# Transposing the gathered rows of routed expert tiles by DMA in two 16-bit planes, and the last 32 rows of an output projection as one stacked float32r product

## The chip, the cores and the metric

The kernel runs on one core of one Trainium2 chip. Its time is the device time of an execution in microseconds; lower is better. The engines are PE (TensorE), DVE (VectorE), ACT (ScalarE), POOL (GpSimd) and SP (SyncE, which here only issues transfers). L-numbers are lines of the kernel before.

## The reference, cut to what matters

There are N = 625 rows of D = 1024 float32 numbers and 20000 edges. A graph layer comes first, then an expert layer:

```python
# graph layer, on h = layernorm(x), n = t5_layer_norm(h)
out = n @ W_root + bias
for r in range(2):                        # mean of the messages of each relation
    sums = segment_sum((n[src] @ W_rel[r]) * (type == r)[:, None], dst)
    out += sums / maximum(count, 1)[:, None]
x = x + h + elu(out) @ wo                 # wo: 286 x 1024, the output projection

# expert layer, on h2 = layernorm(x)
shared = mean over 2 of  gelu(h2 @ sW1 + sb1) @ sW2 + sb2
moe    = sum over the top 2 of 8 experts of  w_e * (gelu(h2 @ W1[e] + b1[e]) @ W2[e] + b2[e])
x = x + h2 + shared + moe
```

The rows choose their experts by a gate computed at run time, so which rows meet which weights is known only then.

## The kernel before, in words

**Graph part.** Rows stand in NT = 5 tiles of TP = 125. PE counts the edges into a matrix (`cnt`), multiplies the normed rows by the three 286-column weights (`project`, L907), and aggregates by the counts (`aggregate`, L924, whose operands are float32r). `count_out` writes the counts with ACT copies. `elu(d)` makes a tile of activations of 286 columns, `elu_columns(d)` transposes it on PE into `eT`.

**Output projection.** `output_proj(d)` (L962) multiplies `eT` by `wo`. The first 256 rows of `wo` go as two float32 products per 512-column half (L967). The remaining 30 rows go as a pair of 30-row products, one for each half (L971), at two different row offsets of the array. DVE then adds the result to `xh` (L974), takes its statistics, and scales it (`layernorm`, L729; its square root is on ACT, L721) into `h2`. POOL issues the DMAs that store `h2` to the DRAM tensor `h2d` and `xh` to `x1d` (L980, L981). `to_columns(d)` transposes `h2` on PE (L808) and ACT copies the transposes to `h2T` (L816). The loop of L1070 emits `output_proj(s)` and then `to_columns(s - 2)`.

**Routing.** While PE multiplies the shared experts' first weights (`shared_in`, L1163), DVE finds for each row its two experts and the slot it takes. The result `tok` (L1282) lists, for each of NJ = 11 tiles of 128 slots, which row sits in each slot. `bias_parts` uses a buffer of the pool `io`, called `b2x`.

**Routed experts, first product.** The loop of L1409 runs over the 11 tiles. `fetch(j)` has POOL gather the 128 rows of a tile from `h2d` into `xs` (pool `io`, 3 buffers), PE transposes the eight 128x128 blocks into PSUM (`p_x`, L1366), and ACT and DVE copy four blocks each to `xsT` (L1372, L1370; pool `xt`, 2 buffers). `expert_in(j)` multiplies (`p_h`, L1385); DVE copies the result to `hj`. `expert_mid(j)` transposes that on PE (`p_hT`, L1397) and ACT applies gelu into `hjT` (L1400). PE's order is: transposes of tile n+1, product of tile n, transposes of `hj` of tile n-1. ACT also makes copies of weights, `w1m` (L1379), for tiles that hold more than one expert.

**The rest.** The second product of the routed experts (`p_yj`, L1443), a scatter of its rows to DRAM, the shared experts' second product (`p_o`, L1498), the sum and the stores. Pools are given back and reused as the stages end: the pool `xt` lies where the shared experts' inputs were.

Of the kernel before, what the change touches and what calls it, by code (L numbers as in the profile page):

```python
# [18 lines left out]
N = 625  # L19
D = 1024  # L20
# [433 lines left out]
def sparse_kernel(  # L454
# [32 lines left out]
    banks_of = ExitStack()  # L487
    psum, nacc = [banks_of.enter_context(tc.tile_pool(name="psum", bufs=1, space=bass.MemoryType.PSUM))], [3]
    dram = ctx.enter_context(tc.tile_pool(name="dram", bufs=1, space=bass.MemoryType.DRAM))
    h2d = dram.tile([N, D], F32, name="h2d")  # L490
    x1d = dram.tile([N, D], F32, name="x1d")

    yt = dram.tile([2 * YB, D], F32, name="yt")
# [17 lines left out]
    crow = pool(cnts, "crow", 2)  # L511
    front = ExitStack()
    fbig = pool(front, "fbig", side="right")
    oneh = pool(front, "oneh", 6, side="right")


    PARTS = (slice(0, 112), slice(112, TP))
# [303 lines left out]


    CT = cbig.tile([TP, NT, R * N], F32R, name="CT")
    def count_out(d, n, acc):
        xi = crow.tile([TP, R * WD], I32, tag="xi", name=f"xi_{d}")[:, : R * n]
        nc.scalar.activation(xi, acc[:, : R * n], AF.Copy, scale=256.0)
        five = [TP, NT, R * n]
        ct = crow.tile([TP, NT, R * WD], I32, tag="ct", name=f"ct_{d}")[:, :, : R * n]
        nc.vector.tensor_tensor(ct, xi[:, None, :].to_broadcast(five),
                                mask[:, :, None].to_broadcast(five), op=ALU.bitwise_and)  # L830
        for r in range(R):
            nc.scalar.copy(CT[:, :, r * N + d : r * N + d + n], ct.rearrange("p t (d r) -> p t d r", r=R)[:, :, :, r])

# [66 lines left out]
    agg = gbig.tile([TP, NT, F], F32, name="agg")  # L900


    def project(i):
        r, m = divmod(i, NT)
        p = ps_acc(f"p_pr_{m}_{r}")
        for k in range(KD):
            nc.tensor.matmul(p[:TP, :F], nT[:, k, m * TP : (m + 1) * TP], wg[:, k, r, :],  # L907
                             start=(k == 0), stop=(k == KD - 1))
        if r < R:
            rest = crow.tile([TP, F], F32, tag="rest", name=f"rest_{m}_{r}")  # L910
            nc.scalar.activation(rest, p[:TP, :F], AF.Copy, scale=sc2[:, 1, m : m + 1])
            nc.scalar.copy(P[:, m, r, 0, :F], rest)
            nc.vector.tensor_sub(P[:, m, r, 1, :F], rest, P[:, m, r, 0, :F])
        else:
            nc.vector.scalar_tensor_tensor(agg[:, m, :], p[:TP, :F], sc2[:, 0, m : m + 1], cb,
                                           op0=ALU.mult, op1=ALU.add)

    def aggregate(d, r):

        p = (ps_acc if r and d in (1, 3, 4) else ps_mm)(f"p_agg_{d}_{r}")  # L920
        at = r * N + d * TP
        for m in range(NT):
            for i in range(2):
                nc.tensor.matmul(p[:TP, : F + 2], CT[:, m, at : at + TP], P[:, m, r, i],  # L924
                                 start=(m == 0 and i == 0), stop=(m == NT - 1 and i == 1))
        nc.scalar.copy(deg[:, R * d + r : R * d + r + 1], p[:TP, F : F + 1])
        inv = small.tile([TP, 2], F32, tag="inv", name=f"inv_{d}_{r}")
        nc.vector.tensor_scalar(inv[:, 0:1], p[:TP, F : F + 1], 1.0, None, op0=ALU.max)
        nc.vector.reciprocal(inv[:, 1:2], inv[:, 0:1])
        nc.vector.scalar_tensor_tensor(agg[:, d, :], p[:TP, :F], inv[:, 1:2], agg[:, d, :],  # L930
                                       op0=ALU.mult, op1=ALU.add)

    els = {}

    def elu(d):
        z = agg[:, d, :]
# [12 lines left out]
    def elu_columns(d):  # L949
        p = ps_mm(f"p_elT_{d}")  # L950
        pv = p[:, : 3 * TP].rearrange("p (k n) -> p k n", k=3)
        eT = grow.tile([128, 3, TP], F32, tag="eT", name=f"eT_{d}", bufs=NT - 1)
# [5 lines left out]
        eTs[d] = eT  # L958

    h2s = {}  # L960

    def output_proj(d):  # L962
        eT = eTs[d]
        ps = [ps_acc(f"p_y_{d}_{s}") for s in range(2)]
        for s in range(2):
            for k in range(2):
                nc.tensor.matmul(ps[s][:TP, :], eT[:, k, :], wo_t[:, k, s * 512 : (s + 1) * 512],  # L967
                                 start=(k == 0), stop=False)
        for s in range(2):
            r = slice(s * QC, s * QC + FL)  # L970
            nc.tensor.matmul(ps[s][:TP, :], eT[r, 2, :], wo_r[r], start=False, stop=True)  # L971
        for s in range(2):
            at = slice(s * 512, (s + 1) * 512)
            nc.vector.tensor_add(xh[:TP, d, at], xh[:TP, d, at], ps[s][:TP, :])  # L974
# [25 lines left out]
    def at(c, f, *args):  # L1000
        after[c].append((f, args))
# [3 lines left out]
            at(c0, stats, t + 1)  # L1005
        at(c1, to_columns, t + 1, None, nT, True)

    zero = fbig.tile([128, D // 2], F32, name="zero")

    def clear():  # L1010
        nc.gpsimd.memset(zero, 0.0)
        for a in range(2):
# [341 lines left out]
    xsT, p_hs, w1m = {}, {}, {}  # L1354

    def fetch(j):
        xs = io.tile([128, D], F32, tag="io", name=f"xs_{j}")
        nc.gpsimd.indirect_dma_start(  # L1358
            out=xs, out_offset=None, in_=h2d,
            in_offset=bass.IndirectOffsetOnAxis(ap=tok[:, j : j + 1], axis=0))  # L1360
        t_ = xt.tile([128, KD, 128], F32, tag="xsT", name=f"xsT_{j}")
        for g in range(2):
            p = ps_acc(f"p_x{g}_{j}")
            for k in range(4):
                at = (4 * g + k) * 128
                nc.tensor.transpose(p[:, k * 128 : (k + 1) * 128], xs[:, at : at + 128], ident)  # L1366
# [182 lines left out]
```

## Time and profile before

| | |
|---|---|
| median of 3 runs | 298.02 us (296.13 to 298.16) |
| the profiled execution's own time | 298.92 us |
| its span, first to last instruction | 297.2 us |
| mean granted TensorE clock | 0.994 |
| PE busy, of the span | 286.6 us, 96% |
| DVE, ACT, POOL busy | 166.1, 102.0, 43.9 us |
| output projection and its transposes | 97.3 to 131.2 us of the span |
| shared experts' first product | to 165.0 us |
| routed experts' first product | 165.0 to 216.0 us |
| bytes moved by DMA in that last stage | 84 GB/s on the mean |

The profile is of one execution. Its page gives busy times, a picture of the span in 40 slices, the chain of work that ended last, and groups of equal instructions. The chain can also be read piece by piece, with the start, the length and the line of each piece. A group's row gives the line, the engine, what is written from what, the count, the busy time with the mean of one, and the idle time of the engine before them with what ended it. In the chain a float32 matmul counts as two PE instructions.

### The profile page before, as it was taken

What the parts mean: (1) busy time and instruction counts of PE and PEld (TensorE: products, weight loads), DVE (VectorE), ACT (ScalarE), POOL (GpSimd) and SP (SyncE); (2) the same over time, 40 slices, a digit from 0 to 9 for tenths busy, and PEclk for the clock granted to TensorE, in tenths of its full rate; (3) what the DMA queues carried; (4) which work ended last, traced back from release to release, by engine and by line L of the source; (5) the groups of instructions that cost most, each with busy time, mean ns of one, the idle gap of its engine ahead of it and who ended that gap; (6) DMA issues with size and microseconds to landing.
All of it is one profiled execution on the core that took longest, in us unless ns stands there. A gap on an engine that the chain in (4) does not pass through costs nothing.

```text
span 297.2 us, 4546 instructions
## 1 busy us (share of the span) xinstructions
PE 286.6 (96%) x1583; PEld 190.7 (64%) x1583; DVE 166.1 (56%) x458; ACT 102.0 (34%) x236; POOL 43.9 (15%) x97
## 2 busy tenths in 40 slices
PE   7988999999999999999999999999999999999991
PEld 5866777788888434567777887788743334444451
DVE  6779999997664588838980222132133211157920
ACT  2338424413542322335132543646289111000000
POOL 9500000000000034322021221110012222200000
PEclk9999999999999999999999999999999999999997
DMA  6999920000000999999999433420086545399351
GB/s 218 333 311 391 408 87 1 3 0 2 0 0 23 342 366 394 392 390 375 356 409 409 163 112 125 131 82 2 2 306 247 210 192 225 138 354 370 136 156 45
DMA packets 28658, 61.01 MB, mean 205 GB/s; under 512 B 2177, under 2 KB 16008, under 8 KB 28625
## 3 DMA queue, kind: packets, MB, share of 16 engines
q1 hardware_dynamic: 23102, 43.77, 41.4%
q0 software_dynamic: 5232, 16.55, 15.1%
q10 hardware_dynamic: 296, 0.35, 0.5%
q8 instruction: 15, 0.25, 0.4%
q14 instruction: 13, 0.10, 0.1%
HBM read 42.62 MB, written 18.81 MB: 207 GB/s over the span
## 4 chain that ended last, share of the span: by engine, by line
PE 87%; DMA 4%; DVE 4%; ACT 2%; SPq 1%; issue 0%; ACTq 0%
PE p_pr L907 17%; PE p_h L1385 13%; PE p_yj L1443 13%; PE p_o L1498 12%; PE p_sh L1163 11%; PE p_y L967 6%; PE p_agg L924 5%; DMA xh<-in_x_dram 4%; PE p_x L1366 3%; PE p_y L971 2%; PE cnt L885 1%; PE p_t L808 1%; PE p_hT L1397 1%; DVE st L765 1%; PE p_gate L1111 1%; PE p_o L1500 1%
## 5 line engine op out<-in xcount | busy, mean ns | idle before, releaser
L907 PE MATMUL p_pr<-wg,nT 128*125 128x286 f32 x240 | 61.8, 409 | 1.4 <-ACT nT L814 0.9
L907 PEld LDWEIGHTS p_pr<-wg,nT 128*125 128x125 f32 x240 | 43.6, 187 | 14.1 <-ACT nT L814 2.2
L1385 PE MATMUL p_h<-w1a,xsT 128*128 (+2 forms) x176 | 40.0, 380 | 0.0
L1443 PE MATMUL p_yj<-w2a,hjT 128*128 (+2 forms) x88 | 38.6, 594 | 0.0
L1498 PE MATMUL p_o<-sw,shT 128*125 128x512 f32 (+1 forms) x88 | 36.1, 553 | 0.0
L1163 PE MATMUL p_sh<-h2T,sw 128*128 128x313 f32 (+1 forms) x128 | 35.2, 429 | 0.0
L1385 PEld LDWEIGHTS p_h<-w1a,xsT 128*128 128x128 f32 (+2 forms) x176 | 28.8, 168 | 7.4 <-issue 0.5
L1163 PEld LDWEIGHTS p_sh<-h2T,sw 128*128 128x128 f32 x128 | 23.7, 190 | 8.6 <-issue 0.2
L1443 PEld LDWEIGHTS p_yj<-w2a,hjT 128*128 128x128 f32 (+2 forms) x88 | 14.4, 168 | 22.4 <-issue 22.4
L1498 PEld LDWEIGHTS p_o<-sw,shT 128*125 128x125 f32 x88 | 16.4, 188 | 16.9 <-issue 16.2
L1447 DVE COPY ys<-p_yj 128x512 f32<-128x512 f32 x15 | 10.4, 692 | 28.7 <-PE p_yj L1443 27.1
L1389 DVE COPY hj<-p_h 128x256 f32<-128x256 f32 x11 | 4.7, 425 | 30.8 <-PE p_h L1385 30.8
L981 POOL DMA_DIRECT2D x1d<-xh x10 | 5.4, 539 | 94.4 <-DVE flagf L710 91.3
L1451 POOL DMA_INDIRECT yt<-ys,row x11 | 10.8, 981 | 50.5 <-DVE ys L1447 50.5
L967 PE MATMUL p_y<-wo_t,eT 128*125 128x512 f32 x40 | 18.0, 593 | 0.0
L1358 POOL DMA_INDIRECT xs<-h2d,tok x11 | 10.6, 962 | 45.6 <-PE p_x L1366 30.9
L1370 DVE COPY xsT<-p_x 128x512 f32<-128x512 f32 x11 | 7.6, 692 | 17.4 <-PE p_x L1366 14.7
L1400 ACT ACTIVATE hjT<-p_hT,vT 128x128 f32<-128x128 f32 (+2 forms) x34 | 8.7, 332 | 24.5 <-PE p_hT L1397 24.5
L1474 DVE SCALAR_TENSOR_TENSOR x<-p_o,x 125x512 f32<-125x512 f32 (+1 forms) x11 | 6.9, 641 | 16.3 <-PE p_o L1500 16.3
L924 PE MATMUL p_agg<-P,CT 125*125 125x288 f32 x100 | 15.5, 305 | 0.0
L1385 PE MATMUL p_h<-w1m,xsT 128*64 128x256 f32 (+1 forms) x96 | 14.7, 382 | 0.0
L1443 PE MATMUL p_yj<-w2m,hjT 128*64 128x512 f32 (+1 forms) x48 | 14.1, 595 | 0.0
(306 smaller groups left out, 413.9 us busy)
## 6 DMA issues: line engine op xcount, KB each, us to landing
w1a<-in_L_ffn_W_dram SPq DMA_DIRECT2D x8, 1024.0 KB
w2a<-in_L_ffn_W_dram SPq DMA_DIRECT2D x8, 1024.0 KB, 7.0
yt<-zero SPq DMA_DIRECT2D x2, 2560.0 KB
g<-yt SPq DMA_DIRECT2D x10, 512.0 KB, 7.5
sw<-in_L_ffn_sW_dram SPq DMA_DIRECT2D x4, 1024.0 KB, 6.8
x<-x1d SPq DMA_DIRECT2D x5, 500.0 KB
x1d<-xh POOLq DMA_DIRECT2D x5, 448.0 KB, 6.6
h2d<-h POOLq DMA_DIRECT2D x5, 448.0 KB, 6.2
```

The source lines that it names most:

```text
L907: nc.tensor.matmul(p[:TP, :F], nT[:, k, m * TP : (m + 1) * TP], wg[:, k, r, :], start=(k == 0), stop=(k == KD - 1))
L924: nc.tensor.matmul(p[:TP, : F + 2], CT[:, m, at : at + TP], P[:, m, r, i], start=(m == 0 and i == 0), stop=(m == NT - 1 and i == 1))
L967: nc.tensor.matmul(ps[s][:TP, :], eT[:, k, :], wo_t[:, k, s * 512 : (s + 1) * 512], start=(k == 0), stop=False)
L1163: nc.tensor.matmul(p[:, : z - a], sw1[:, i, k, t * 128 : (t + 1) * 128], h2T[:, k, a:z], start=(k == 0), stop=(k == KD - 1))
L1358: nc.gpsimd.indirect_dma_start(out=xs, out_offset=None, in_=h2d, in_offset=bass.IndirectOffsetOnAxis(ap=tok[:, j : j + 1], axis=0))
L1366: nc.tensor.transpose(p[:, k * 128 : (k + 1) * 128], xs[:, at : at + 128], ident)
L1385: nc.tensor.matmul(p[a:b, :H], xsT[j][:, k, a:b], w1m[j, a][:, 0, k, :] if a else w1a[:, bass.ds(e, 1), k, :], start=(k == 0), stop=(k == ...
L1400: nc.scalar.activation(hjT[:, j, t, a:b], p[:, t * 128 + a : t * 128 + b], AF.Gelu, bias=bT[:, bass.ds(e, 1), t])
L1443: made = nc.tensor.matmul(p[a:b], hjT[:, j, k, a:b], w2m[j, a, k][:, at] if a else w2a[:, bass.ds(e, 1), k, at], start=(k == 0), stop=(k = ...
L1447: nc.vector.tensor_copy(y[:, at], p)
L1451: sent.append(nc.gpsimd.indirect_dma_start(out=yt, out_offset=bass.IndirectOffsetOnAxis(ap=row[:, j : j + 1], axis=0), in_=y, in_offset=No ...
L1498: nc.tensor.matmul(p[:TP, :n], shT[:, i, k, own], sw2[:, i, k, at], start=(i == 0 and k == 0), stop=False)
```

## The change

Three things are done together.

1. `h2d` holds each row as two 16-bit planes: ACT splits `h2` into low and high halves of its numbers (a new tile `hp`, two ACT copies per tile of 125 rows), and POOL stores `hp`. A gathered tile `xs` is then 128 rows of 2048 16-bit numbers. The SP queue transposes it with two DMA transposes per tile, of 1024 columns each, into `xq` (2 buffers). DVE copies the low plane of each half and ACT the high plane, interleaved, to `xsT`. PE's eight transposes per tile and their PSUM buffers go.
2. The last 32 rows of `wo` (254 to 285) are loaded four times below each other into a tile of 128 rows and split into float32r parts, once (`last_rows`, one ACT copy and one DVE instruction). `elu` repeats the last 32 columns, `elu_columns` makes a float32r tile `eR` of them, with a DVE subtraction for the lower 64 rows, and `output_proj` adds one float32r product of 128 rows per half in place of the 30-row product.
3. Buffers are given up for it: `io` has 2 instead of 3, `oneh` 5 instead of 6, `agg` is used for the four copies of the rows of `wo` before it holds sums, and `zero` is declared earlier.

```diff
-    h2d = dram.tile([N, D], F32, name="h2d")
+    h2d = dram.tile([N, 2 * D], I16, name="h2d")
-    oneh = pool(front, "oneh", 6, side="right")
+    oneh = pool(front, "oneh", 5, side="right")
...
-    FL = F - 256
+    FL = F - QC
     nc.sync.dma_start(wo_t, wo[:256].rearrange("(t p) m -> p t m", p=128))
-    wo_r = gbig.tile([2 * QC, 512], F32, name="wo_r")
-    for s in range(2):
-        nc.sync.dma_start(wo_r[s * QC : s * QC + FL], wo[256:, s * 512 : (s + 1) * 512])
+    agg = gbig.tile([128, NT, F], F32, name="agg")
+    wo_4 = agg.rearrange("p t f -> p (t f)")[:, :D]
+    nc.sync.dma_start(wo_4, bass.AP(tensor=wo.tensor, offset=wo.offset + FL * D,
+                                    ap=[[0, 4], [D, QC], [1, D]]))
+    wo_r = gbig.tile([128, D], F32R, name="wo_r")
+    less = fbig.tile([128, 1], F32, name="less")
+    for g in range(4):
+        nc.gpsimd.memset(less[g * QC : (g + 1) * QC], -float(g % 2))
+
+    def last_rows():
+        with tc.issue_after(outs[-1].ins):
+            nc.scalar.copy(wo_r, wo_4)
+        nc.vector.scalar_tensor_tensor(wo_r, wo_r.bitcast(F32), less, wo_4, op0=ALU.mult, op1=ALU.add)
...
     def elu(d):
...
-        el = grow.tile([TP, 256 + 2 * QC], F32, tag="el", name=f"el_{d}", bufs=3)
-        nc.vector.memset(el[:, 256:], 0.0)
+        el = grow.tile([TP, FL + 128], F32, tag="el", name=f"el_{d}", bufs=3)
...
-        nc.scalar.copy(el[:, 256 + QC : F + QC], el[:, 256:F])
+        nc.scalar.copy(el[:, F:].rearrange("p (g f) -> p g f", g=3),
+                       el[:, FL:F][:, None, :].to_broadcast([TP, 3, QC]))
...
     def elu_columns(d):
...
-        for k in range(3):
-            n = min(128, 256 + 2 * QC - k * 128)
-            nc.tensor.transpose(pv[:n, k, :], els[d][:, k * 128 : k * 128 + n], ident[:TP, :TP])
-        nc.scalar.copy(eT[:, :2], pv[:, :2])
-        nc.scalar.copy(eT[: 2 * QC, 2], pv[: 2 * QC, 2])
+        eR = grow.tile([128, TP], F32R, tag="eR", name=f"eR_{d}", bufs=NT - 1)
+        for k, a in enumerate((0, 128, FL)):
+            nc.tensor.transpose(pv[:, k, :], els[d][:, a : a + 128], ident[:TP, :TP])
+        nc.scalar.copy(eT, pv[:, :2])
+        nc.scalar.copy(eR, pv[:, 2])
+        nc.vector.tensor_sub(eR[64:], pv[64:, 2], eR[64:])
...
     def output_proj(d):
...
         for s in range(2):
+            at = slice(s * 512, (s + 1) * 512)
             for k in range(2):
-                nc.tensor.matmul(ps[s][:TP, :], eT[:, k, :], wo_t[:, k, s * 512 : (s + 1) * 512],
-                                 start=(k == 0), stop=False)
-        for s in range(2):
-            r = slice(s * QC, s * QC + FL)
-            nc.tensor.matmul(ps[s][:TP, :], eT[r, 2, :], wo_r[r], start=False, stop=True)
+                n = min(128, FL - k * 128)
+                nc.tensor.matmul(ps[s][:TP, :], eT[:n, k, :], wo_t[:n, k, at], start=(k == 0), stop=False)
+            nc.tensor.matmul(ps[s][:TP, :], eR, wo_r[:, at], start=False, stop=True)
...
         h2s[d] = h2
+        hp = planes.tile([TP, 2, 2, D // 2], I16, tag="hp", name=f"hp_{d}")
+        for g in range(2):
+            nc.scalar.copy(hp[:, g], h2[:, g * 512 : (g + 1) * 512].bitcast(I16).rearrange("p (d b) -> p b d", b=2))
         for g in PARTS:
             at = slice(d * TP + g.start, d * TP + g.stop)
-            nc.gpsimd.dma_start(h2d[at, :], h2[g, :])
+            nc.gpsimd.dma_start(h2d[at, :], hp[g].rearrange("p g b d -> p (g b d)"))
...
+    at(100, last_rows)
...
+            planes = pool(gnn, "planes", 2)
...
-    io = pool(ctx, "io", 3)
+    io = pool(ctx, "io", 2)
...
     def fetch(j):
-        xs = io.tile([128, D], F32, tag="io", name=f"xs_{j}")
+        xs = io.tile([128, 2 * D], I16, tag="io", name=f"xs_{j}")
         nc.gpsimd.indirect_dma_start(
             out=xs, out_offset=None, in_=h2d,
             in_offset=bass.IndirectOffsetOnAxis(ap=tok[:, j : j + 1], axis=0))
         t_ = xt.tile([128, KD, 128], F32, tag="xsT", name=f"xsT_{j}")
+        o = t_.bitcast(I16).rearrange("p k (n b) -> p b k n", b=2)
         for g in range(2):
-            p = ps_acc(f"p_x{g}_{j}")
-            for k in range(4):
-                at = (4 * g + k) * 128
-                nc.tensor.transpose(p[:, k * 128 : (k + 1) * 128], xs[:, at : at + 128], ident)
-            o = t_[:, 4 * g : 4 * g + 4, :]
-            pv = p.rearrange("p (k n) -> p k n", k=4)
-            if g:
-                nc.vector.tensor_copy(o, pv)
-            else:
-                copied = nc.scalar.copy(o, pv)
+            xq = xt.tile([128, 2, KD // 2, 128], I16, tag="xq", name=f"xq_{j}_{g}")
+            nc.sync.dma_start_transpose(xq.rearrange("p b k n -> p (b k) n"), xs[:, g * D : (g + 1) * D])
+            k = slice(4 * g, 4 * g + 4)
+            nc.vector.tensor_copy(o[:, 0, k], xq[:, 0])
+            copied = nc.scalar.copy(o[:, 1, k], xq[:, 1])
         xsT[j] = t_
```

More of the change, by code (lines that the diff above doesn't have):

```diff
@@ L655, in sparse_kernel @@
     wo_t = gbig.tile([128, 2, D], F32, name="wo_t")
-    FL = F - 256
+    FL = F - QC
     nc.sync.dma_start(wo_t, wo[:256].rearrange("(t p) m -> p t m", p=128))
-    wo_r = gbig.tile([2 * QC, 512], F32, name="wo_r")
-    for s in range(2):
-        nc.sync.dma_start(wo_r[s * QC : s * QC + FL], wo[256:, s * 512 : (s + 1) * 512])
+    agg = gbig.tile([128, NT, F], F32, name="agg")
[10 more added lines that the diff above has]
+        nc.vector.scalar_tensor_tensor(wo_r, wo_r.bitcast(F32), less, wo_4, op0=ALU.mult, op1=ALU.add)
+    zero = fbig.tile([128, 512], F32, name="zero")
     nc.vector.tensor_scalar(low[:, 1], low[:, 0], 1.0 / DEG, 0.5 / DEG - 0.5, op0=ALU.mult, op1=ALU.add)
@@ L823, in sparse_kernel @@
     CT = cbig.tile([TP, NT, R * N], F32R, name="CT")
+    outs = []
     def count_out(d, n, acc):
@@ L831, in count_out @@
         for r in range(R):
-            nc.scalar.copy(CT[:, :, r * N + d : r * N + d + n], ct.rearrange("p t (d r) -> p t d r", r=R)[:, :, :, r])
+            outs.append(nc.scalar.copy(CT[:, :, r * N + d : r * N + d + n],
+                                       ct.rearrange("p t (d r) -> p t d r", r=R)[:, :, :, r]))
     nil = fbig.tile([1, 512], BF16, name="nil")
@@ L899, in sparse_kernel @@
         nc.gpsimd.memset(P[:, m, :, 0, F:].bitcast(F32), 16.0 ** -m)
-    agg = gbig.tile([TP, NT, F], F32, name="agg")
     def project(i):
@@ L914, in project @@
         else:
-            nc.vector.scalar_tensor_tensor(agg[:, m, :], p[:TP, :F], sc2[:, 0, m : m + 1], cb,
+            nc.vector.scalar_tensor_tensor(agg[:TP, m, :], p[:TP, :F], sc2[:, 0, m : m + 1], cb,
                                            op0=ALU.mult, op1=ALU.add)
@@ L929, in aggregate @@
         nc.vector.reciprocal(inv[:, 1:2], inv[:, 0:1])
-        nc.vector.scalar_tensor_tensor(agg[:, d, :], p[:TP, :F], inv[:, 1:2], agg[:, d, :],
+        nc.vector.scalar_tensor_tensor(agg[:TP, d, :], p[:TP, :F], inv[:, 1:2], agg[:TP, d, :],
                                        op0=ALU.mult, op1=ALU.add)
@@ L935, in elu @@
     def elu(d):
-        z = agg[:, d, :]
+        z = agg[:TP, d, :]
         lo = grow.tile([TP, F], F32, tag="lo", name=f"lo_{d}")
@@ L951, in elu_columns @@
         pv = p[:, : 3 * TP].rearrange("p (k n) -> p k n", k=3)
-        eT = grow.tile([128, 3, TP], F32, tag="eT", name=f"eT_{d}", bufs=NT - 1)
-        for k in range(3):
-            n = min(128, 256 + 2 * QC - k * 128)
-            nc.tensor.transpose(pv[:n, k, :], els[d][:, k * 128 : k * 128 + n], ident[:TP, :TP])
-        nc.scalar.copy(eT[:, :2], pv[:, :2])
-        nc.scalar.copy(eT[: 2 * QC, 2], pv[: 2 * QC, 2])
-        eTs[d] = eT
+        eT = grow.tile([128, 2, TP], F32, tag="eT", name=f"eT_{d}", bufs=NT - 1)
+        eR = grow.tile([128, TP], F32R, tag="eR", name=f"eR_{d}", bufs=NT - 1)
[4 more added lines that the diff above has]
+        nc.vector.tensor_sub(eR[64:], pv[64:, 2], eR[64:])
+        eTs[d] = eT, eR
     h2s = {}
     def output_proj(d):
-        eT = eTs[d]
+        eT, eR = eTs[d]
         ps = [ps_acc(f"p_y_{d}_{s}") for s in range(2)]
         for s in range(2):
+            at = slice(s * 512, (s + 1) * 512)
             for k in range(2):
-                nc.tensor.matmul(ps[s][:TP, :], eT[:, k, :], wo_t[:, k, s * 512 : (s + 1) * 512],
-                                 start=(k == 0), stop=False)
-        for s in range(2):
-            r = slice(s * QC, s * QC + FL)
-            nc.tensor.matmul(ps[s][:TP, :], eT[r, 2, :], wo_r[r], start=False, stop=True)
+                n = min(128, FL - k * 128)
+                nc.tensor.matmul(ps[s][:TP, :], eT[:n, k, :], wo_t[:n, k, at], start=(k == 0), stop=False)
+            nc.tensor.matmul(ps[s][:TP, :], eR, wo_r[:, at], start=False, stop=True)
         for s in range(2):
@@ L1006, in sparse_kernel @@
         at(c1, to_columns, t + 1, None, nT, True)
-    zero = fbig.tile([128, D // 2], F32, name="zero")
     def clear():
```

## The prediction

> **What bounds the kernel now.** I read the page's busy times first, then its chain of work by engine.
>
> ```profile
> span 297.2 us, 4546 instructions
> PE 286.6 (96%) x1583; PEld 190.7 (64%) x1583; DVE 166.1 (56%) x458; ACT 102.0 (34%) x236; POOL 43.9 (15%) x97
> ...
> PE 87%; DMA 4%; DVE 4%; ACT 2%; SPq 1%; issue 0%; ACTq 0%
> ```
>
> PE is busy 96% of the span and is 87% of the chain: PE work taken out shortens the kernel only while nothing else falls in behind it. Next, the same chain piece by piece (start, length, piece) over the stage with the removed transposes:
>
> ```profile
> 159.77 5.26 PE p_sh L1163 x20
> 165.03 1.75 PE p_x L1366 x16
> 166.77 3.46 PE p_h L1385 x16
> 170.23 0.87 PE p_x L1366 x8
> 171.10 3.46 PE p_h L1385 x16
> 174.56 0.22 PE p_hT L1397 x2
> 174.78 0.87 PE p_x L1366 x8
> ...
> 212.05 3.59 PE p_h L1385 x64
> 215.64 0.37 PE p_hT L1397 x2
> 216.01 0.86 PE p_yj L1443 x2
> ```
>
> PE runs without a gap from 165.03 to 216.01. A tile costs 3.46 to 3.60 (`p_h`) + 0.87 (`p_x`) + 0.22 to 0.37 (`p_hT`), some 4.6 us.
>
> The third view is the chain over the output projection, and the fourth the timeline of DVE there:
>
> ```profile
> 117.63 1.00 PE p_t L808 x8
> 118.63 3.44 PE p_y L967 x8
> 122.07 1.10 PE p_y L971 x4
> ```
>
> ```profile
> 117.66 0.69 DVE L974 TENSOR_TENSOR xh<-xh,p_y 125x512 f32<-125x512 f32 x1 [0.56 <-PE p_y L971]
> ...
> 123.15 0.69 DVE L974 TENSOR_TENSOR xh<-xh,p_y 125x512 f32<-125x512 f32 x1 [0.50 <-PE p_y L971]
> ```
>
> PE needs 3.44 + 1.05 + 1.00 = 5.49 us per tile. DVE works on each tile for all but 0.16 to 0.56 us of that, so it stands close behind.
>
> **Output projection: cheaper on PE, then bound by DVE.** The 30-row pair costs 1.05 per tile. A float32r matmul of 288 columns takes 1.40/10 = 0.14 us in the chain (`p_agg`, L924), so one of 512 columns 0.14 x 512/288 = 0.25, and two 0.50. PE saves 0.55 x 5 = 2.8 us. The first tile gives its 0.55 in full; after that DVE's idle times before L974 are all that can be recovered: 0.16 + 0.28 + 0.56 + 0.50 = 1.5. That is 2.05. Against it stand ten new ACT copies `hp`, 2 per tile, of 1024 elements per partition; the nearest row, the bfloat16 copy of L646, takes 1.04. In the built program they stand on ACT ahead of the next tile's square root, for which DVE waits: `hp` of tile d starts once tile d-1 is copied to `h2T`, and 2.1 us later comes the square root. I lay this out tile by tile and find it 0.1 to 0.3 late on two tiles. I take 1.8 gained; bounds 0.5 (the copies late each time) and 2.8. The shared product then ends at 165.03 - 1.8 = 163.2 instead of 165.03. `h2d` is written 2 us later than `h2` was, at some 137, and is needed by the first gather at 149.2: covered by 10 us of `p_sh`.
>
> **One-time work: nothing.** `last_rows` (1.04 on ACT, 1.28 on DVE, by L1434 and L796), three memset-like edits, the wider copy in `elu`, the DVE subtraction on 64 rows in `elu_columns`, one `oneh` buffer less: all lie near 57 to 97 us, where PE's row stands at nine tenths or more and DVE's at four to nine. Without that cover it would be 2 us; I count 0, and -0.5 to +1 for the range.
>
> **Routed stage: what goes.** PE loses 11 x 0.87 = 9.6 us. With PE alone as bound the stage would end at 163.2 + (216.0 - 165.0 - 9.6) = 204.6.
>
> **What comes.** A tile now goes gather, two DMA transposes, copies, product. Three waits of the built program matter.
> (a) `xq` lies where the shared experts' inputs were: the first transpose waits for the last `p_sh` matmul, at 163.2. PE, which used to start `p_x` right there, waits for a whole transpose and a copy.
> (b) `xq` has two buffers, one tile's worth: a transpose of tile n+1 waits for the DVE and ACT copies of the same half of tile n.
> (c) `io` has two buffers: the gather of tile n+2 waits until both transposes of tile n are done. Queued behind it on POOL are only later gathers; behind a waiting transpose on SP only later transposes.
>
> The gather's own time is shown, from its issue:
>
> ```profile
> DMA to landing us min/median/max: 4.1/4.7/8.9
> ```
>
> With the semaphores around it I take 4.9. It was hidden by a third buffer: POOL's timeline has them issued 8 to 13 us ahead of their PE transposes.
>
> **Price of a transpose.** No row shows one. Call L the time from issue to landing of one half (128 x 1024 numbers of two bytes, 256 KB) and D the time by which the second half lands later. Low end for D: the bytes at the trace's best slice, 409 GB/s, 0.64 us. High end: the Trainium skill, VectorE: DVE Perf Modes, section "The three transpose paths", gives 1.309 us for one 128x128 block by DMA against 0.39 on TensorE, and its rules send 128x128 transposes to TensorE where PSUM will do. Eight such blocks in a row are 10.5 us. The row and that rule differ much: here a PE transpose of a float32 block costs 0.87/8 = 0.11 us. By the rule read serially the stage would take 11 x 21 us and the kernel near 480; by plain copy speed it would win. The nearest row is SP's own cost of issuing a transfer:
>
> ```profile
> 215.70 0.89 SPq L1422 DMA_DIRECT2D sw<-in_L_ffn_sW_dram  x2
> ```
>
> That is 0.445 each. A transpose here is 64 blocks of 16 rows by 128 columns. The skill (DMA: Bandwidth & Descriptors, in the table on descriptor generation, column for earlier generations) has 512 cycles for a plain transfer and 262,144 for 8,192 transposed blocks, 32 per block. By the trace's 0.445 us a cycle is 0.87 ns, so 64 blocks take 64 x 32 x 0.87 = 1.8 us. This is an estimate; no run shows it yet. I take **D = 1.8**. For L add the fixed part: a 448 KB store lands 3.3 us after issue, 1.1 of it bytes, so 2.1 with the issue. **L = 3.9, L + D = 5.7.**
>
> **The sum.** Wait (c) makes a ring over two tiles: 4.9 + 5.7 = 10.6, or 5.3 us per tile. Wait (b) alone gives L + 0.8 (copy and semaphore) = 4.7; PE alone 3.8. So (c) decides. Tile 0 is transposed at 163.2 + 5.7 = 168.9. Tiles 2, 4, 6, 8, 10 follow at 10.6 each: 221.9. The last tile's first half is there D earlier, 220.1; then copy 0.7, `p_h` 3.6, `p_hT` 0.4: 224.8. Before it was 216.0. The stage ends **8.8 us later**. In general the end is 163.2 + 29.2 + 6(L + D) - D; one us of L is worth six.
>
> DVE and ACT do one more copy of each half: 11 x (2 x 0.69) - 7.6 = +7.6 on DVE (12.1 busy of 51 before) and +6.5 on ACT (25.1 of 51), by L1370 and L1372. Both have room, and the copy's latency of 0.7 is in the sum. If a mode for 2-byte data makes it 0.35, ring (b) gains and (c) does not. PE will stand still for 4.7 us at 163; should its clock drop, `p_h` of tile 0 is longer by at most its own 3.5, and the second tile is not there before 173: covered.
>
> **After it.** The loads of `sw2` and `x1` start as the stage ends and are needed by `p_o` 38 us later, as before. The shift passes to the end whole: 298.92 + 8.8 = 307.7 for an execution like the profiled one, which lies 0.9 above the median of the runs; so **307 us**.
>
> **The rivals.**
> *Quick transposes (faster).* The pages also say (Advanced Engine Details and Errata, "X-Bar Transpose") that such DMAs run like plain ones. With D = 0.6 and L = 2.5 the end is 163.2 + 29.2 + 18.6 - 0.6 = 210.4, a gain of 5.6: **292.5**. It decides from L + D below 3.55, where the gain passes 3 us. For it speaks that the stage moves only 84 GB/s; against it, that L cannot be much under the 2.1 of fixed cost, and that each element lands in two bytes. Floor: PE alone, -11.4, 286.6. Chance 0.25.
> *Break-even.* L + D of 3.55 to 4.6 (D near 1): the freed PE time turns into waiting, 298 within 3 us. Chance 0.10; within 1% is what a measurement of this kernel can about tell from no change.
> *Slow transposes.* D = 3.5, L = 6 (75 GB/s): ring (c) gives 7.2 per tile, the two halves in line 7.0; end 163.2 + 29.2 + 57 - 3.5 = 245.9, kernel **328**. For it speaks the page's 1.309 us per block, against it that 64 blocks can be spread over 16 DMA engines. Chance 0.20.
> *The forecast's case*, L + D of 4.6 to 7.5, 301 to 318: 0.45.
> A rival of another kind, that PE's freed 0.87 is not on the path, is excluded by the gapless chain.
>
> **Range.** 291 to 335: below lie 1 in 20 cases (nearly perfect overlap), above 1 in 10 (L + D over 10.5). Slower by over 1%: 0.45 + 0.20 = 0.65; within 1%: 0.10; faster: 0.25.
>
> **What would show it.** After the last `p_sh` PE idles 4 to 5 us, waiting for a copy of `xsT`; then 1 to 2 us before each `p_h`. Gathers wait for DMA transposes, not for DVE or ACT, and come in step with them, 5.3 us apart. The transposes' landing time is L. `p_y` with the stacked product takes 3.9 per tile, and the last `p_sh` ends 1 to 2.5 us earlier. If PE has no gaps between tiles, the forecast is wrong by its price L + D; if the idle time before `p_h` ends on ACT or DVE copies that waited for buffers, the ring was misread.

## The result, and the profile after

| | before | after |
|---|---|---|
| median of 4 runs each, on one chip | 298.09 us (296.13 to 298.25) | 320.25 us (317.42 to 324.36) |
| ratio, 95% interval | | 1.073 (1.068 to 1.079) |
| profiled execution: own time, span | 298.92, 297.2 us | 320.70, 318.7 us |
| mean granted TensorE clock | 0.994 | 0.975 |
| first product of the routed experts | 165.03 to 216.01 | 158.69 to 237.04 |

The changed kernel is 7.3% slower. The ratio leaves out the changed kernel's slow run of 324.36 us. The forecast was 307 us, 3.0% slower: the direction holds, the size is less than half of what came. L-numbers are now lines of the changed kernel, which stand 11 to 17 higher than in the kernel before; in the views of a run further below they are lines of that run's kernel.

The head of the page of the changed kernel (busy times, then the chain of work by engine):

```profile
span 318.7 us, 4469 instructions
PE 280.5 (88%) x1485; PEld 183.2 (57%) x1485; DVE 169.6 (53%) x470; ACT 122.0 (38%) x258; POOL 44.3 (14%) x101
...
PE 60%; DMA 21%; DVE 11%; ACT 3%; SPq 2%; issue 1%; ACTq 0%
```

PE fell from 87% of the chain to 60%, and transfers rose from 4% to 21%. PE is busy 6 us less, and the kernel takes 22 us more: PE now waits, and most of what was added to the chain is transfers.

The chain of work over the routed stage of the changed kernel (start, length, piece; pieces called issue, under 0.1 us, are left out), where before there was PE without a gap:

```profile
154.97 3.69 PE p_sh L1179 x14
...
166.64 5.62 DMA xq<-xs
172.29 0.77 ACT xsT L1384
...
173.09 5.01 DMA xq<-xs
178.12 0.77 ACT xsT L1384
178.89 0.65 SPq L1381
...
179.70 5.46 DMA xq<-xs
185.18 0.77 ACT xsT L1384
...
185.97 6.99 DMA xq<-xs
192.97 0.77 ACT xsT L1384
193.74 0.84 SPq L1381
...
237.04 0.86 PE p_yj L1455 x2
```

It goes to and fro between a DMA transpose and the ACT copy that frees the buffer it wrote. Printed like this it looks like wait (b) of the prediction, the `xq` ring, and no gather (`xs`) stands in it. From 166.64 to 220.87 it takes eight steps, 6.8 us each; the transposes in these steps, each the second of its tile, last 5.01 to 6.99 from issue to landing, 5.7 on the mean.

In every other step, though, a piece of SP follows the copy (0.65 at 178.89, 0.84 at 193.74): the buffer was free, and SP was still issuing the first transpose of the same tile. Why SP was late, its own waits show (155 to 240; who waited for what: us in total, times, longest):

```profile
SPq L1381 <- DMA xs<-h2d,tok: 36.0, 9, 5.6
...
SPq L1381 <- ACT xsT L1384: 3.3, 8, 0.7
```

Nine times SP stood for a gather, 4 us each; its eight waits for ACT copies add up to 3.3. That is wait (c), the ring of two gather buffers. The printed chain puts each step down to one releaser, here the copy, and so misses what had held up the transfer before it in SP's line.

The waits of the other engines, 155 to 245:

```profile
POOL xs L1374 <- DMA xq<-xs: 56.4, 9, 8.5
ACT xsT L1384 <- DMA xq<-xs: 39.4, 17, 5.1
PEld p_h L1397 <- ACT xsT L1384: 17.1, 8, 7.0
```

PE waits for the copies, the copies for transposes, and the gathers on POOL for transposes too. POOL's timeline shows when the gathers are issued:

```profile
165.88 0.93 POOL L1374 DMA_INDIRECT xs<-h2d,tok  x1 [8.48 <-DMA xq<-xs]
173.03 0.94 POOL L1374 DMA_INDIRECT xs<-h2d,tok  x1 [6.22 <-DMA xq<-xs]
...
215.34 0.94 POOL L1374 DMA_INDIRECT xs<-h2d,tok  x1 [6.10 <-DMA xq<-xs]
```

From 165.88 to 215.34 there are seven steps, 7.07 us each. And these are SP's issues of the transposes of the tiles with numbers 3 and 4, counted from 0, both halves (start, time from the first to the end of the second):

```profile
178.31 2.66 SPq L1381 DMA_TRANSPOSE xq<-xs  x2
184.31 2.90 SPq L1381 DMA_TRANSPOSE xq<-xs  x2
```

One turn of ring (c) can be read from these lines. The gather of tile 3 is issued at 173.03 and SP can issue that tile's first transpose at 178.31; the second follows at 179.70 and lands 5.46 later, at 185.16; then the gather of tile 5 is issued. The tiles with odd numbers go on like this to the ninth with no wait for a copy. The even ones have their second transpose held by a copy as well, by 0.4 us at most. So ring (c) sets the pace, and ring (b) is nearly as slow.

The second thing to see is the moment: each gather starts when the transposes of a tile land, which is when the second transpose of the next tile is issued (165.88 beside 166.64, 173.03 beside 173.09). These two are always in flight together.

The output projection went the other way. Its chain in the changed kernel:

```profile
112.17 0.86 PE p_t L819 x8
113.03 1.72 PE p_y L983 x4
114.75 0.23 PE p_y L984
```

A tile takes 2 x (1.72 + 0.23) = 3.90 of `p_y` in place of 3.44 + 1.05 = 4.49. The stacked float32r product is 0.23. PE runs on from one tile to the next as before.

Where the 21.8 us between the two profiled executions are:

| | us |
|---|---|
| start of the first `p_y`, 97.59 to 94.78 | -2.8 |
| first `p_y` to last `p_y`, 25.6 to 22.1 | -3.4 |
| last `p_y` to last `p_sh` | -0.1 |
| routed stage, 51.0 to 78.35 | +27.4 |
| from there to the end of the span, 81.2 to 81.7 | +0.5 |
| outside the span | +0.3 |

The first line is not the change: the first rows of `x` came 9.91 us after their issue instead of 12.73, and runs of the unchanged kernel on one chip differ by as much (295.47 to 298.79). In the runs below that have the new product, the first `p_y` starts anywhere from 94.4 to 98.5.

### The profile page after: what moved, and what is told of

Its sections match the earlier page's. It is cut to its first block, busy times and chain, and to the rows that moved or that the text cites. A ratio compares the mean times of both kernels' runs of the same rounds, so it can differ in the third digit from the quotient of the medians.

```text
span 318.7 us, 4469 instructions
## 1 busy us (share of the span) xinstructions
PE 280.5 (88%) x1485; PEld 183.2 (57%) x1485; DVE 169.6 (53%) x470; ACT 122.0 (38%) x258; POOL 44.3 (14%) x101
## 4 chain that ended last, share of the span: by engine, by line
PE 60%; DMA 21%; DVE 11%; ACT 3%; SPq 2%; issue 1%; ACTq 0%
DMA xq<-xs 18%; PE p_yj L1455 12%; PE p_sh L1179 11%; PE p_o L1510 11%; PE p_pr L920 9%; PE p_y L983 5%; PE p_agg L937 4%; DMA xh<-in_x_dram 3%; PE p_h L1397 3%; DVE ohs L873 2%; ACT xsT L1384 2%; DVE ohs L874 2%; PE p_t L819 1%; DVE st L776 1%; DVE xh L807 1%; DVE ohk L877 1%
## 5 line engine op out<-in xcount | busy, mean ns | idle before, releaser
L1397 PE MATMUL p_h<-w1a,xsT 128*128 (+2 forms) x176 | 47.3, 423 | 28.3 <-ACT hjT L1412 14.4
L1397 PEld LDWEIGHTS p_h<-w1a,xsT 128*128 128x128 f32 (+2 forms) x176 | 31.7, 188 | 41.6 <-ACT xsT L1384 17.1
L1383 DVE COPY xsT<-xq 128x512 int16<-128x512 int16 x22 | 10.0, 457 | 63.7 <-DMA xq<-xs 63.7
L1384 ACT COPY xsT<-xq 128x512 int16<-128x512 int16 x22 | 16.8, 764 | 40.5 <-DMA xq<-xs 39.4
L1455 PEld LDWEIGHTS p_yj<-w2a,hjT 128*128 128x128 f32 (+2 forms) x88 | 14.4, 168 | 22.4 <-issue 22.4
L983 PE MATMUL p_y<-wo_t,eT 128*125 128x512 f32 (+1 forms) x40 | 18.8, 592 | 0.0
L1397 PE MATMUL p_h<-w1m,xsT 128*64 128x256 f32 (+1 forms) x96 | 16.8, 404 | 0.0
L1455 PE MATMUL p_yj<-w2m,hjT 128*64 128x512 f32 (+1 forms) x48 | 14.1, 595 | 0.0
L874 DVE TENSOR_TENSOR ohs<-ohs,cols 125x1024 f16<-125x1024 f16 (+1 forms) x22 | 13.9, 630 | 0.0
```

Source lines behind the costliest of these rows:

```text
L874: last = nc.vector.tensor_tensor(os, os, both(VV_, 128)[1], op=ALU.mult)
L983: nc.tensor.matmul(ps[s][:TP, :], eT[:n, k, :], wo_t[:n, k, at], start=(k == 0), stop=False)
L1384: copied = nc.scalar.copy(o[:, 1, k], xq[:, 1])
L1397: nc.tensor.matmul(p[a:b, :H], xsT[j][:, k, a:b], w1m[j, a][:, 0, k, :] if a else w1a[:, bass.ds(e, 1), k, :], start=(k == 0), stop=(k == ...
L1455: made = nc.tensor.matmul(p[a:b], hjT[:, j, k, a:b], w2m[j, a, k][:, at] if a else w2a[:, bass.ds(e, 1), k, at], start=(k == 0), stop=(k = ...
```

## The experiments

The theory was this: the transposes are not slow alone; gathers and transposes share the DMA engines, which draws out both, and with two `xq` buffers (ring (b)) each drawn-out transpose is paid in full. The rivals were that a DMA transpose takes 5 to 7 us whatever runs beside it, and that the two gather buffers (ring (c)) set the pace, as the prediction had it.

Times are of one run unless said otherwise. "Stage" is from the end of the last `p_sh` to the first `p_yj`, "step" the mean time from one gather to the next once the stage runs (without gathers, and where PE sets the pace, from one `p_h` tile to the next).

| run | us | stage | step |
|---|---|---|---|
| changed kernel | 320.25 (median of 4) | 78.4 | 7.1 |
| stacked product only | 294.07 (median of 5) | 51.0 | 4.6 |
| transposes only | 323.49 | 75.8 | 7.1 |
| nine of eleven gathers left out | 296.52 | 55.1 | 4.5 |
| plain copies instead of transposes | 304.03 | 61.7 | 5.3 |
| room alone (control) | 321.34 | 76.1 | 7.0 |
| three gather buffers | 314.98 | 71.5 | 6.4 |
| four `xq` buffers | 306.94 | 63.0 | 5.4 |
| both | 304.28 | 60.5 | 5.3 |
| both, first transposes meant to start early | 304.88 | 59.1 | 5.2 |
| both, first two tiles with room of their own | 304.80 | 60.6 | 5.4 |

Stages with the same buffers came out as 78.4, 76.1 and 75.8, and three of the changed kernel's four times lie within 3.3 us: smaller differences between single runs say nothing.

### The two halves of the change alone

The stacked product alone: the kernel before with the new `wo_r`, `last_rows`, `elu`, `elu_columns` and the new product.

```diff
-            r = slice(s * QC, s * QC + FL)
-            nc.tensor.matmul(ps[s][:TP, :], eT[r, 2, :], wo_r[r], start=False, stop=True)
+            nc.tensor.matmul(ps[s][:TP, :], eR, wo_r[:, at], start=False, stop=True)
```

> The stacked float32r product alone, with gathers and PE transposes as before. If the two parts add up, this keeps what the changed kernel gains ahead of the transposes: 5 x (1.05 - 0.46) = 2.95 us of PE in the output projection, so 294.5 to 295.5 us, and the last shared matmul ends 3 to 4 us before 165.03. If the first rows of x also landed 3 us earlier in the changed kernel because of this part and not by chance, 292. Rival: DVE stands behind PE and takes the gain back, as the prediction had it: 296.3, the last shared matmul 1.8 us earlier.

Measured: 294.07 us (5 runs) against 297.81 (7 runs of the kernel before, same chip), ratio 0.990, 95% interval 0.984 to 0.996. So this half gains 3.7 us, some 1%, and is faster than both kernels. The rival's 296.3 lies inside the interval, at its edge; in the trace the stretch from the first `p_y` to the last is 3.4 us shorter than before, as in the changed kernel, so DVE takes nothing back there.

The transposes alone: the changed kernel with the output projection of before.

> The DMA transposes alone, with the output projection of before. If the parts add up: 320.3 + 3 = 323 us, and the stage from the last shared matmul to the first matmul of the second expert product takes the 78 us of the changed kernel. Rival: the early end of the projection made the first transposes collide with the last weight loads, and with a later start the stage is shorter: below 75 us.

Measured: 323.49. Against 297.81 that is +25.7, and +25.7 - 3.7 = +22.0 is the result of both (+22.2). The halves add up, and the loss is all in the routed stage. Its stage of 75.8 lies between the 78 expected and the rival's 75. The control run further below has 76.1 with the new product in it, so the rival is not needed to explain a difference of 2 us.

### Taking the gathers away

```diff
+    held = []
     def fetch(j):
-        xs = io.tile([128, 2 * D], I16, tag="io", name=f"xs_{j}")
-        nc.gpsimd.indirect_dma_start(...)
+        if len(held) < 2:
+            xs = io.tile(...); nc.gpsimd.indirect_dma_start(...); held.append(xs)
+        else:
+            held.append(held[-2])
+            xs = held[-1]
```

> Left out: the gathers of nine of the eleven tiles; they transpose the rows of the first two tiles again. Sharing theory (gather and transposes of one tile run on the same 16 DMA engines at the same time and slow each other): a transpose lands in 3.1 to 3.5 us, the step from tile to tile falls from 7.1 to 4.5 to 5.0 us, kernel near 298. Rival, slow by itself (a transpose takes 5 to 6 us whoever else moves): the step stays at 6.5 to 7, kernel 314 to 319. Rival, the gather's ring of the prediction alone, no sharing: the step is L + 0.8 = 6.4 with the L of 5.6 seen, kernel 313.

Measured: 296.52 us, a stage of 55.1. The same 22 transposes are there. From the chain of this run:

```profile
185.01 3.06 DMA xq<-xs
188.09 0.78 ACT xsT L1390
188.88 4.47 DMA xq<-xs
```

Once the weight loads are over, the transposes in this chain land in 3.06 to 4.47 us, with the other half of their tile in flight for part of that time. With a gather beside them, second transposes took 5.0 to 7.0. The changed kernel has the same contrast in itself: its last transpose is issued at 229.10, when the last gather (issued at 221.27) has landed, and DVE copies its result from 232.23 on, 3.1 us later. So a transpose is not slow by itself, and 23 us of the stage go with the gathers. The step is 4.5. PE alone would need 51.0 - 9.6, some 41 us for the stage (an estimate), so the transposes and their copies still hold PE up. This run takes away the gather ring as well as the sharing; the runs with more buffers below tell these two apart.

### The same bytes without the transposition

```diff
-            nc.sync.dma_start_transpose(xq.rearrange("p b k n -> p (b k) n"), xs[:, g * D : (g + 1) * D])
+            nc.sync.dma_start(xq.rearrange("p b k n -> p (b k n)"), xs[:, g * D : (g + 1) * D])
```

> Left out: the transposing; each DMA transpose is a plain copy of the same 256 KB from and to the same buffers. Shape theory (the transpose's 256-byte pieces keep the engines busy 1.7 us where plain rows would take 0.65): the step per tile falls from 7.1 to 4.5 to 5 us, kernel 295 to 302. Rival, latency (issue, landing, buffers; the shape does not matter): the step stays above 6, kernel over 310.

Measured: 304.03, stage 61.7, a step of 5.3. This misses what the theory had, by 2 us in the time. The chain shows why:

```profile
175.47 5.03 DMA xs<-h2d,tok
...
180.63 3.40 DMA xq<-xs
...
191.69 5.37 DMA xs<-h2d,tok
```

Here the gather stands in the chain, and the ring of two gather buffers sets the step. So quick transfers on these buffers would still have left the stage some 11 us longer than before.

What the form of the transfer costs is read from the queues' rows on the pages (packets, MB, share of 16 engines over the span). First the run with the stacked product alone, which moves nothing into `xq`:

```profile
q1 hardware_dynamic: 23144, 44.17, 42.4%
q0 software_dynamic: 5232, 16.55, 15.4%
```

then the changed kernel:

```profile
q1 hardware_dynamic: 46376, 49.94, 50.3%
q0 software_dynamic: 5232, 16.55, 15.2%
```

then plain copies:

```profile
q1 hardware_dynamic: 26312, 49.94, 46.3%
```

and the run without nine gathers:

```profile
q1 hardware_dynamic: 46376, 49.94, 54.1%
q0 software_dynamic: 3936, 11.83, 10.3%
```

For q1, share times span gives 123.1, 160.3 and 139.9 us of all sixteen engines in the first three. Over 22 transfers of 256 KB the packets of a transpose occupy them for (160.3 - 123.1)/22 = **1.69 us**, those of a plain copy for (139.9 - 123.1)/22 = 0.76. The transposes also make 22 x 1024 packets of 256 bytes. A gather in the changed kernel occupies them for (48.4 - 30.3)/9 = **2.0 us**.

These times are not quite fixed costs. A gather with no transposes beside it takes (44.7 - 30.3)/9 = 1.6, a transpose with no gathers (159.3 - 123.1)/22 = 1.65. A tile therefore needs 2 x 1.65 + 1.6 = **4.9 us of all sixteen engines** by the lower figures and **5.4** by those of the changed kernel. PE's whole step with its own transposes was 4.6.

### More buffers

The buffers need room. It was made by keeping seven of the eight second weights and using those of expert 0 in every second product. All the runs from here on have that edit; the control has nothing else.

```diff
-    w2a = pool(ctx, "w2a").tile([128, NE, HK, D], F32, name="w2a")
+    w2a = pool(ctx, "w2a").tile([128, NE - 1, HK, D], F32, name="w2a")
```

> The control for the three runs that had more buffers: the changed kernel with only the edit that made room for them (seven of the eight second weights kept, the second product always with those of expert 0, so the routed rows of the output are other numbers; the buffers are those of the change, io 2 and xq 2). Every theory expects it like the changed kernel: 318 to 323, some 7 us from transpose to transpose. Near 315 or under it the room itself would have been part of the gain of the runs with more buffers.

Measured: 321.34, stage 76.1, gathers 7.0 apart. The room by itself gains nothing.

Three gather buffers:

```diff
-    io = pool(ctx, "io", 2)
+    io = pool(ctx, "io", 3)
```

> The changed kernel with a third gather buffer, as before had; the room comes from the second expert weights: seven of eight are kept and the second product of the routed experts takes those of expert 0 for every slot, with the same loads, copies and matmuls. If the gather's ring (gather of tile n+2 waits for the transposes of tile n) sets the step of 7.1 us: the step falls to the xq ring, 5 to 5.5, kernel 298 to 303. If the xq ring alone sets it (transposes of tile n+1 wait for the copies of tile n): no change, 318 to 321. If the sharing of the DMA engines sets it, the earlier gather collides elsewhere and the gain is small: 312 to 318.

Measured: 314.98, stage 71.5, 4.6 us shorter than the control's. In SP's waits no gather is left, so ring (c) is open. The step falls from 7.0 to 6.4 only. The gathers still run beside the transposes, and these are still long:

```profile
200.11 6.13 DMA xq<-xs
206.27 0.77 ACT xsT L1384
207.05 4.64 DMA xq<-xs
```

This is ring (b) alone. The run without nine gathers was ring (b) alone too, with transposes of 3.06 to 4.47 and a step of 4.5. What differs is the gathers in flight: they cost 1.9 us a tile, the wait of ring (c) another 0.6.

Four `xq` buffers:

```diff
-            xq = xt.tile([128, 2, KD // 2, 128], I16, tag="xq", name=f"xq_{j}_{g}")
+            xq = xt.tile([128, 2, KD // 2, 128], I16, tag="xq", bufs=4, name=f"xq_{j}_{g}")
```

> The changed kernel with four xq buffers instead of two, room made in the same way (second product with the weights of expert 0). If the xq ring sets the step: it falls to the gather's ring, (5.8 + 3.1 + 1.5)/2 = 5.2 to 6, kernel 300 to 308. If the gather's ring sets it alone: no change, 318 to 321.

Measured: 306.94, a gain of 14.4 over the control; the stage, 63.0, is 13.1 shorter. Only the wait of a tile's transposes for the copies of the tile before was taken away, so the two `xq` buffers cost more than the two gather buffers. Ring (c) is what is left, now in the chain:

```profile
188.24 5.37 DMA xs<-h2d,tok
...
195.10 3.71 DMA xq<-xs
...
199.57 4.43 DMA xs<-h2d,tok
...
205.48 4.14 DMA xq<-xs
```

Gather, transpose, gather, transpose: two tiles in (199.57 - 188.24) = 11.3 here and in 10.7 on the mean of the stage, where the prediction had 10.6 for this ring and the changed kernel took 14.1. The transfers themselves are shorter than there: a gather lands in 4.7 us (median) in place of 5.8, these transposes in 3.7 and 4.1 in place of 5.7. I read this so: the wait for copies also kept each second transpose beside a gather. No run changed that moment alone.

Both:

> Third gather buffer and four xq buffers together (second product with the weights of expert 0). No buffer is waited for then, and what is left is the DMA engines: 2 x 1.69 us for the transposes and 1.3 us for the gather of each tile, 4.7 us, so a step of 4.7 to 5.2 and a kernel of 295 to 301. If the engines were not the floor, PE would be: a step of 3.8 and 286 to 290. If the step stays above 6, neither buffers nor engine time explain it.

Measured: 304.28, stage 60.5, step 5.3. That misses the 295 to 301 expected, and the step is no better than with four `xq` buffers alone. The rings are wider, not gone: SP still waits for gathers seven times (21.2 us), POOL for transposes eight times (39.9 us). The transfers have become long again. The chain:

```profile
179.17 8.70 DMA xq<-xs
187.90 0.46 DVE xsT L1383
```

The middle of the stage in the changed kernel, in the run with four `xq` buffers, and in this one (columns: stretch, its length, busy time and count of PE, PEld, DVE, ACT and POOL, then the granted clock, the DMA engines' share, GB/s):

```profile
166.00:229.00 63.00, 41.22 (x211) 28.74 (x211) 10.88 (x27) 28.33 (x58) 8.31 (x9) 0.93 0.77 152
```

```profile
166.00:215.00 49.00, 40.48 (x213) 30.52 (x214) 12.69 (x29) 28.60 (x60) 8.44 (x9) 0.90 0.88 194
```

```profile
167.00:212.00 45.00, 36.76 (x199) 27.14 (x200) 11.27 (x27) 26.62 (x55) 7.49 (x8) 0.90 1.16 201
```

From the second to the third the packets' time in flight rises from 0.88 to 1.16 of the sixteen engines (packets overlap, so the sum can pass 1), and the bytes moved only from 194 to 201 GB/s. More in flight, hardly more moved: this speaks for the engines as the last bound. It is not shown beyond that, since the step of 5.3 lies above the 4.9 that a tile needs by the lower figures. The expectation had put this floor at 4.7, with 1.3 for a gather, by bytes; a gather takes 1.6 to 2.0.

### The start of the stage

Two runs tried to transpose the first tiles beside the last `p_sh`. The first gave `xq` a pool of its own:

```diff
+    xqp = pool(xts, "xqp", 4)
```

> As the run before, and the four xq buffers lie in a place that was free already, so that the first transposes need not wait for the last shared matmul (second product with the weights of expert 0). If that wait costs PE its idle time of 5 to 6 us before the first product: that much less than the run before. If the last weight loads hold the first transposes up instead: within 2 us of it.

Measured: 304.88. This edit did not do what it was made for: SP still waited for the last `p_sh` (5.2 us), so the new pool's place still lay over the shared experts' inputs, and the first copy of `xsT` came 6.0 us after it, where it was 6.2 without the edit. The second put the pool where these inputs never were:

```diff
     io = pool(ctx, "io", 3)
+    xqp = pool(ctx, "xqp", 4)
```

> Three gather buffers and four xq buffers as in the run with both, but xq now has room of its own that the shared experts' inputs never used, so the first four transposes (two tiles) can run beside the last p_sh matmuls. Theory (a floor of 5.4 us of the DMA engines per tile, and a start that waits for the last p_sh): tile 0 is copied 0.8 after the last p_sh, tile 2 lands 5.4 after that, tile 10 eight tiles later; with 0.8 + 9 x 5.4 + 3.9 + 0.4 the stage lasts some 54 us in place of 60.5, and the kernel takes 298 (296 to 300). Rival (the DMA engines are not the floor, something else sets 5.4 from tile to tile): only the start is won, 3 us or less, or nothing. If it is PE that follows at 4.6 per tile, the stage comes under 52.

Measured: 304.80, nothing won, as the rival said. Now the first transpose is issued early, at 155.66, 5 us ahead of the last `p_sh`. But SP's part of the chain shows that the engine stood in the issue itself:

```profile
155.66 6.92 SPq L1382
...
162.63 3.33 SPq L1382
...
166.06 1.25 SPq L1382
```

and the trace, with the columns as above, what the transfers met:

```profile
156.00:162.00 6.00, 4.73 (x18) 3.05 (x17) 1.59 (x2) 2.81 (x4) 0.93 (x1) 1.00 1.03 410
```

Eight loads of second weights, 1 MB each, fill the DMA engines at up to 410 GB/s until some 164 us. The transposes go into the same engines. The first `xsT` copy starts at 167.13, 6.4 us after the last `p_sh`. Here, work moved ahead into a stretch in which the DMA engines were full came no earlier. That the full engines are the cause is my reading of these lines: SP issued both, and transposes that wait their turn in a queue behind the weights would look the same. No run had the weights loaded elsewhere. By its own expectation this run does not confirm the floor of 5.4 either.

## Why the prediction was wrong

**The step that failed: the durations in the sum of ring (c), and with them ring (b) as slack.** The prediction took 4.9 for a gather from a stage in which hardly anything ran beside it, and L + D = 5.7 for the transposes of a tile with nothing beside them. It did not ask what the two rings do to each other. In ring (c) a gather starts when transposes land, and in ring (b) the next second transpose starts 0.8 later. The two are thus always in flight together, and each draws out the other. Taken from SP's issues and the landings of the tiles 1 to 9: from a landing to the first transpose of the next tile but one, the gather's 4.9, it was 6.7 on the mean; from there to the landing of the second, L + D, 6.7 to 8.6, with a mean of 7.3. That is 14.0 for two tiles in place of 10.6, and a gather does come 14.1 after the last but one. The prediction's own formula for the stage, 5 gathers + 4.7 + 6(L + D) - D, gives some 80 with these durations instead of 61.6; 78.4 was measured.

Ring (b), put at L + 0.8 = 4.7 and so out of play, became 5.7 + 0.8 = 6.5, close to the 7.1 of the stage. "So (c) decides" is right for the changed kernel as it stands, where SP waits for every gather. But (b) is close behind, and room for it brought more (13.1 us of stage) than room for (c) (4.6), because the transfers became shorter as well. The signs that the prediction named for its ring were met, at a slower beat: gathers wait for transposes, 7.07 apart instead of 5.3, and PE's idle time before `p_h` ends on copies that had waited for transposes.

**Term by term.**
- *D = 1.8*, the estimate from SP's issue row: it was worked out from the time of the issuing engine, and that is 1.23 for a transpose against 0.47 for a plain copy. Without gathers the copies of the two halves start 0.7 to 2.7 apart, mostly 1.1 to 1.5; in the changed kernel, beside gathers, 2.1 to 4.6.
- *L = 3.9*: too high without a gather (mostly 3.1 to 3.6), too low for a second transpose beside a gather (5.0 to 7.0). (In its fixed part 3.3 - 1.1 is 2.2, not 2.1.)
- *Gather 4.9*: from issue to landing the median was 4.7 before, and is 5.8 for the changed kernel's eleven.
- *Output projection 1.8*: 3.4 to 3.7. The prediction took DVE's idle times as all that PE could recover. DVE did not hold PE up: PE passed through all five tiles without a gap, and where DVE's last statistics were late, PE had `p_sh` matmuls to run (118.03 and 119.68 in its chain). A matmul of the stacked product is 0.23, as estimated (0.25), and PE's saving of 2.95 was realised in full. The wider and reordered work on ACT cost PE one wait of 0.2.
- *PE's stand of 4.7 at the start, clock covered*: PE stood 6.5 us; between 162 and 170 the granted clock was 0.57, against 1.00 ahead of it, and the first `p_h` took longer. In the changed kernel this hid behind the next transpose, as said. In the run without gathers it did not: its first 32 `p_h` instructions took 9.81 us where 2 x 3.46 = 6.92 is usual: 2.9 us more, in the chain.
- *The shift passes to the end whole*: right, 81.2 before and 81.7 after.

**The rivals.** Quick transposes (292.5) are ruled out: even plain copies gave 304. Slow transposes (328, with L = 6 and 7.2 per tile) had the numbers that came, but by luck: there the transposes were slow by themselves. The Trainium skill's 1.309 us per 128x128 block (VectorE: DVE Perf Modes, "The three transpose paths") read serially is 10.5 us for eight, and a transpose of eight such blocks landed in 3.06 without a gather beside it. The opposite rule, that these transfers run like plain ones (Advanced Engine Details and Errata, "X-Bar Transpose (TRN2)"), does not hold here either: 1.69 us of engine time against 0.76. The advice to leave 128x128 transposes to TensorE where PSUM will do (VectorE: DVE Perf Modes, "Rules for kernel authors") was right for this kernel: the transposes of a tile cost 2 x 1.69 = 3.4 us of the DMA engines, and 0.87 of PE.

**Could the idea be saved?** With all the buffers it wants, which do not fit beside eight second weights, it takes 304; the stacked product without it takes 294.07. The DMA engines need 4.9 to 5.4 per tile for gather and transposes, PE needed 4.6 for everything. A division, with some of the blocks left to PE, was not tried.

## What to carry to other kernels

When work goes from an engine to DMA, first add up what the sixteen DMA engines need per turn of the loop, gathers and all, and compare that with the engine's own step; here it was 4.9 to 5.4 against 4.6, once a run had given the price of a transpose. Then draw the rings of buffers and ask which transfers they start at the same moment: a duration taken from a quiet stage does not hold there, and it enters every turn. When the chain names one wait, look also at what the issuing engine itself waited for; a ring of nearly the same length can hide behind the one that is printed. On the other side, a second engine that "stands close behind" is no limit while the first has other work to fill in, as the output projection showed.

## What the runs showed of the hardware

- A DMA transpose of 128 x 1024 16-bit numbers within SBUF is 1024 packets of 256 bytes and takes the sixteen engines 1.65 to 1.69 us (155 GB/s), a plain copy of the same bytes 0.76. A gather of 128 rows of 4 KB takes them 1.6 us alone and 2.0 beside transposes.
- The row of SP for them, over the whole stage of the changed kernel (duration min, median, max in ns, first and last start):

```profile
L1381 SPq DMA_TRANSPOSE xq<-xs x22: 1231/1233/3066, 158.7 to 229.1; - x22
```

  The issue takes 1.23 us in the median. Beside the loads of weights, at 410 GB/s, issues took 6.92 and 3.33 us in the last run: the issuing engine's time for such a transfer is not fixed.
- A copy that interleaves 16-bit numbers, 128 x 512, took ACT 0.76 us and DVE 0.46. The prediction's 0.69 from a 4-byte row was too high for DVE and a little low for ACT.
